# A list scheduler that lets the sums of VectorE and GpSimd exclude each other, and weight sums moved from the attention to the experts

## The chip, the cores and the metric

The kernel runs on one core of a Trainium2 chip. The metric is the device time of one execution in microseconds (us). Five engines work side by side in it, each with its own queue that is worked off in order: TensorE (PE in the profile, with its weight loads as PEld), VectorE (DVE), ScalarE (ACT), GpSimd (POOL) and SyncE (SP), which issues nearly all DMAs. They wait for each other through semaphores.

## The reference

Two transformer layers over 32 sequences of 128 positions with 512 features, all in fp32. The first layer normalises, adds a shift made from the condition, does attention with 16 heads of 64, and then a mixture of eight experts, in which every expert takes the 512 tokens that score highest for it. The second layer is an adaptive-norm block with attention (16 heads of 32) and an MLP of width 2048.

```python
# layer 0
h = _ln(x) + silu(t) @ W_ada.T
q, k, v = h @ Wqkv.T            # q and k normalised per head
x = x + softmax(q k^T / 8) v @ Wout.T
gate = softmax(tok @ Wgate.T);  vals, idx = top_k(gate.T, bs // 8)
y = gelu_tanh(_ln(tok[idx]) @ fc1[e].T) @ fc2[e].T
tok = tok.at[idx].add(y * vals)
# layer 1
n = layernorm(x) * (1 + scale) + shift
x = x + softmax(q k^T / sqrt(32)) v @ wo.T + bo
n = layernorm(x) * (1 + scale2) + shift2
x = x + gelu(n @ w1.T + b1) @ w2.T + b2
```

## The kernel before

**Stages.** The profiled execution goes through the attention of the first layer (0 to about 1000 us, called attention below), a short routing stage, eight experts (about 1110 to 1900 us, about 99 us each), and the second layer (about 1920 us to the end). The second layer works on eight blocks of four sequences. A block is two groups of two sequences (`group(g)`: norm, q/k/v, softmax, output projection, second norm), then `up(G, ...)` (first MLP matrix and gelu) and `down(G, ...)` (second MLP matrix). In the steady part a block takes about 161 us, and the attention of the next block is laid between the MLP products of this one.

**Fewer products, more sums.** Every large matrix product is made from 2x2 blocks with seven block products instead of four times two, at the price of sums of blocks on both sides. In the second layer's MLP this is done twice, one level inside the other: 49 products of four 128x128 matmuls each for `up` (`seeded`, L2794) and 49 for `down` (`chained`, L2876). So TensorE has less to do, and VectorE and GpSimd have much: sums of operands, sums of weights, and the combining of products. Sums of two tensors in SBUF go through `tt` (L1270): it gives the scheduler one way for VectorE (L1273) and, where allowed, one for GpSimd (L1274). In `down`, four such sums (`sums`, L2912) are made for each of seven outer products `o`; they are bound to GpSimd and held back by a gate on earlier products, `inner_done[-(2)]`: from the third outer product on, the sums may not begin before block product 7 of the chain two back is done.

**Weight sums of the last layer.** The summed forms of `w1` and `w2` don't depend on the data. They are made once, in 22 steps (`w1_outer`, `w2_outer`, `w1_inner`, `w2_inner`): each step loads four 128x512 pieces (`fetch`), makes four sums on GpSimd (`weight_forms`, through `tt`), and stores the results to DRAM (`put`), from where the second layer streams them (`piece`, L2696). That is 88 loads, 88 sums and 100 stores of 256 KB. In this kernel they belong to jobs 3 to 13, which lie in the first layer's attention.

**The order is planned.** All work is recorded as operations with an engine, an assumed duration, what they read and write, a priority (lower goes first) and a job number. `Sched.run` then plays them through in Python at build time: of all operations that could go it takes the one that can start earliest by its own clock, emits it, and so fixes the order of each engine's queue. Some operations may go to either of two engines; the plan chooses. On the chip nothing of the plan's times is left, only the order in each queue and the semaphores for true dependencies. The plan's durations are simple lines in the number of elements:

```python
def mm_us(n, count=1):
    return count * 2 * max(2 * n / 2400 + 0.0025, 0.11)
TR = 0.11
def dve_us(n, ptrs=0, half=False):
    return 0.15 + n / (1920 if half else 960) + 0.06 * ptrs
```

In the second layer a switch (`side_by_side`) gives `tt` other durations, for VectorE and GpSimd running beside each other: `0.15 + n / 700` and `0.16 + n / 400`, which is 0.88 and 1.44 us for 512 elements.

**Names for later.** `newton` (L419) makes an inverse root from the variance by an initial guess (L424) and three rounds of three tiny VectorE instructions (L428, L430, L432) on 128x2 or 128x4 elements. `normed` feeds it the variance (L464). `norm_T` (L2452) uses the result to scale rows (L2457), TensorE transposes them (L1243), and their columns are scaled and moved out of PSUM by VectorE or ScalarE (L2467, L2469). `chain_T` (L2565) makes the v and output projections; its results are taken up by L2588 and L2660 on VectorE. `comb` (L2721) and its copies on ScalarE (L2717) do so for `down`.

Of the kernel before, what the change touches and what calls it, by code (L numbers as in the profile page):

```python
# [14 lines left out]
ALU = mybir.AluOpType  # L15
# [171 lines left out]
class Op:  # L187
    __slots__ = ("alts", "prio", "job", "keep", "deps", "n", "ready", "next", "bufs", "lat", "done", "table", "seq", "mb")


class Sched:
# [7 lines left out]
    def __init__(self, window):  # L199
        self.ops, self.window = [], window  # L200
        self.load_exp = None

    def op(self, eng, us, fn, w=(), r=(), prio=0.0, job=0, keep=0, spare=0, lat=0.0, table=None, also=(), share=1.0):
# [4 lines left out]
        o = Op()  # L208
        o.alts = {eng: (us, fn)}
# [39 lines left out]
    def run(self):  # L249
# [10 lines left out]
        table = None  # L260
        live = set()
# [33 lines left out]
        while left:  # L295
            best = None
            for e in ENGINES:
# [3 lines left out]
                for o in cand[e]:  # L301
# [3 lines left out]
                    at = max(at, o.ready, free[e])  # L305
                    us = o.alts[e][0]
# [27 lines left out]
            free[e] = end  # L334
            lat = o.lat
# [24 lines left out]
def mm_us(n, count=1):  # L360

    return count * 2 * max(2 * n / 2400 + 0.0025, 0.11)


TR = 0.11
# [14 lines left out]
class Stage:  # L380
# [38 lines left out]
    def newton(self, v, n, name, pr, job):  # L419
# [7 lines left out]
        for _ in range(3):  # L427
            sch.op(DVE, us, lambda: nc.vector.scalar_tensor_tensor(t.t, y.t, -0.5, y.t, ALU.mult, ALU.mult),  # L428
                   w=[t], r=[y], prio=pr, job=job)
            sch.op(DVE, us, lambda: nc.vector.tensor_tensor(t.t, t.t, v.t, ALU.mult),  # L430
                   w=[t], r=[t, v], prio=pr, job=job)
            sch.op(DVE, us, lambda: nc.vector.scalar_tensor_tensor(y.t, t.t, 1.5, y.t, ALU.add, ALU.mult),  # L432
                   w=[y], r=[t, y], prio=pr, job=job)
        return y

    def guessed(self, mv, v, n, name, pr, job):
# [11 lines left out]
               w=[t], r=[y], prio=pr, job=job)  # L448
        sch.op(DVE, us, lambda: nc.vector.tensor_tensor(t.t, t.t, v.t, ALU.mult),
               w=[t], r=[t, v], prio=pr, job=job)  # L450
        sch.op(DVE, us, lambda: nc.vector.scalar_tensor_tensor(y.t, t.t, 1.5, y.t, ALU.add, ALU.mult),
               w=[y], r=[t, y], prio=pr, job=job)
# [701 lines left out]
def fast_kernel(ctx: ExitStack, tc: tile.TileContext, x, condT, mask, cols, w_ada, wqkv, wout, wout_p, wout_o, wgate,  # L1154
# [113 lines left out]
    side_by_side = [False]  # L1268

    def tt(o_, a_, b_, op_, n, w, r, pr, job, first=DVE, also=True):  # L1270

        shared = side_by_side[0]
        ways = {DVE: (DVE, 0.15 + n / 700 if shared else dve_us(n), lambda: nc.vector.tensor_tensor(o_(), a_(), b_(), op_)),  # L1273
                POOL: (POOL, 0.16 + n / 400 if shared else pool_us(n), lambda: nc.gpsimd.tensor_tensor(o_(), a_(), b_(), op_))}  # L1274
        sch.op(*ways[first], also=[ways[POOL if first == DVE else DVE]] if also else (), w=w, r=r, prio=pr, job=job)

    def recip(inv, ps, pr, job, at=None):
# [7 lines left out]
        if kept:  # L1285
# [5 lines left out]
               w=[inv], r=[t, y], prio=pr, job=job)  # L1291
# [951 lines left out]
    fence_b = stands(fence)  # L2243
    for e in range(E):
        up_done, near_end = expert(e, [fence_b] if e else [])

# [76 lines left out]
    def fetch(b_, src, r, pr, job):  # L2323
        sch.op(SP, 0.06, lambda: nc.sync.dma_start(b_.t, src), w=[b_], r=r, lat=4.0, prio=pr, job=job, spare=12)
# [68 lines left out]
    for n, step in enumerate(steps):  # L2393
        job = 3 + n // 2
# [659 lines left out]
```

## Time and profile before

The time is 3243.3 us (median of three runs, 3242.47 to 3243.88). The profiled execution took 3246.01 us, with a span of 3244.3 us from its first to its last instruction.

| stretch (us) | what | PE busy | DVE busy | ACT busy | POOL busy | GB/s |
|---|---|---|---|---|---|---|
| 0 to 1000 | attention, layer 0 | 962.5 | 786.3 | 364.3 | 235.6 | 124 |
| 1000 to 1120 | routing | 115.6 | 99.0 | 8.2 | 8.8 | 181 |
| 1120 to 1880 | experts | 759.1 | 515.0 | 174.5 | 495.1 | 111 |
| 1880 to 2000 | start of layer 1 | 117.4 | 59.1 | 40.8 | 6.3 | 62 |
| 2000 to 3140 | layer 1 | 1094.8 | 871.4 | 555.7 | 420.1 | 176 |
| 3140 to end | last block | 84.5 | 60.7 | 36.0 | 60.2 | 207 |

The columns are microseconds in which an engine had at least one instruction under way. A matmul's end is modelled, so a busy PE need not be PE at its peak; a gap in PE is a real gap. A group's mean duration can hide two cases, the instruction that ran alone and the one that was held up, so single instructions in order of time are the view that tells them apart.

### The profile page before, as it was taken

How to read it: one execution, taken by the hardware profiler on the slowest of the kernel's cores; microseconds unless marked ns; L12 is line 12 of the kernel's file. 1: busy time of each engine (PE TensorE's matmuls, PEld its weight loads, DVE VectorE, ACT ScalarE, POOL GpSimd, SP SyncE). 2: the span in 40 equal slices, each digit the busy share in tenths (PEclk: the TensorE clock that was granted, in tenths of full speed). 3: DMA queues.
4: the chain of work that ended last, by engine and by line, in shares of the span. 5: the costliest groups of instructions: out<-in, count | busy, mean ns of one | idle time of the engine just before them, and what ended most of it. 6: DMA issues, size and time to landing. Idle time of an engine off the chain costs nothing. (4 is left out here: it accounts for less than half of the span.)

```text
span 3244.3 us, 60361 instructions
## 1 busy us (share of the span) xinstructions
PE 3134.0 (97%) x22740; PEld 2549.3 (79%) x22740; DVE 2391.5 (74%) x4762; ACT 1179.4 (36%) x2972; POOL 1226.1 (38%) x920
## 2 busy tenths in 40 slices
PE   9999999999999999999999999999999999999997
PEld 5555555555557888888888888999898989898987
DVE  8877777788878897666676546786868686878675
ACT  3333333344431122211222214635353545454533
POOL 0323232221002157766676510615152525151536
PEclk9999999999999999999999999999999999999999
DMA  4234332444135333443333441646465646464666
GB/s 173 98 111 150 105 110 92 166 170 147 50 111 200 127 106 105 115 113 105 104 107 95 129 141 47 208 153 193 154 192 157 191 157 194 152 194 151 195 195 207
DMA packets 293453, 459.99 MB, mean 142 GB/s; under 512 B 29930, under 2 KB 111394, under 8 KB 293154
## 3 DMA queue, kind: packets, MB, share of 16 engines
q1 hardware_dynamic: 284498, 438.43, 42.0%
q0 software_dynamic: 7168, 16.91, 2.8%
q8 instruction: 182, 2.98, 0.4%
q14 instruction: 117, 0.96, 0.1%
q10 hardware_dynamic: 1488, 0.71, 0.1%
HBM read 383.44 MB, written 72.51 MB: 141 GB/s over the span
## 5 line engine op out<-in xcount | busy, mean ns | idle before, releaser
L1274 POOL TENSOR_TENSOR base<-base,base 128x512 f32<-128x512 f32 x336 | 466.0, 1401 | 813.6 <-DVE base L2845 473.3
L2876 PE MATMUL bank<-base,base 128*128 128x128 f32 x3072 | 375.1, 280 | 10.9 <-DVE base L2721 8.2
L1273 DVE TENSOR_TENSOR base<-base,base 128x512 f32<-128x512 f32 (+2 forms) x471 | 362.6, 788 | 30.3 <-ACT base L2737 9.5
L2876 PEld LDWEIGHTS bank<-base,base 128*128 128x128 f32 x3072 | 362.4, 195 | 22.9 <-DVE base L2721 11.1
L2794 PE MATMUL bank<-base,base 128*128 128x128 f32 x3088 | 371.8, 277 | 6.2 <-ACT bank L2755 4.9
L2794 PEld LDWEIGHTS bank<-base,base 128*128 128x128 f32 x3088 | 361.3, 193 | 9.6 <-ACT bank L2755 6.0
L2164 PE MATMUL d<-fc,h 128*128 128x256 f32 x992 | 218.9, 379 | 0.0
L2111 ACT ACTIVATE h<-h,prm 128x256 f32<-128x256 f32 x256 | 115.0, 500 | 257.2 <-DVE h L2105 257.1
L2164 PEld LDWEIGHTS d<-fc,h 128*128 128x128 f32 x992 | 188.0, 190 | 25.3
L1467 ACT ACTIVATE sq<-qk 128x512 f32<-128x512 f32 x128 | 81.7, 639 | 297.3 <-DVE qk L1505 257.3
L2100 PE MATMUL u<-gT,fc 128*128 128x256 f32 x768 | 178.6, 382 | 0.5 <-ACT gT L2063 0.5
L2804 ACT ACTIVATE base<-base,prm 128x128 f32<-128x128 f32 x512 | 164.1, 392 | 29.4 <-DVE base L2839 29.3
L2100 PEld LDWEIGHTS u<-gT,fc 128*128 128x128 f32 x768 | 147.2, 192 | 21.4 <-ACT gT L2063 0.9
L2839 DVE TENSOR_TENSOR base<-bank,base 128x512 f32<-128x512 f32 x96 | 65.9, 687 | 96.4 <-PE bank L2794 92.1
L2105 DVE TENSOR_TENSOR h<-v,u 128x512 f32<-128x512 f32 x128 | 86.5, 682 | 49.6 <-PE u L2100 47.9
L2100 PE MATMUL u<-tg,s 128*128 128x256 f32 x512 | 121.0, 379 | 0.9 <-DVE tg L1273 0.9
L1501 PE MATMUL q<-wqkv,hsb 128*128 128x512 f32 x240 | 113.5, 595 | 0.0
L2164 PE MATMUL d<-t,hs 128*128 128x256 f32 x512 | 113.4, 379 | 0.0
L1501 PE MATMUL q<-t,hsa 128*128 128x512 f32 x240 | 112.9, 592 | 0.0
L1501 PE MATMUL q<-wqkv,hT 128*128 128x512 f32 x240 | 111.6, 598 | 0.2 <-DVE hT L1602 0.2
L2845 DVE TENSOR_TENSOR base<-bank,base 128x512 f32<-128x512 f32 x120 | 81.7, 688 | 37.6 <-PE bank L2794 13.3
L2100 PEld LDWEIGHTS u<-tg,s 128*128 128x128 f32 x512 | 97.2, 190 | 14.4 <-issue 1.3
(1150 smaller groups left out, 6693.0 us busy)
## 6 DMA issues: line engine op xcount, KB each, us to landing
base<-w1i SPq DMA_DIRECT2D x224, 256.0 KB, 3.6
base<-w2i SPq DMA_DIRECT2D x224, 256.0 KB, 3.2
base<-w2s SPq DMA_DIRECT2D x168, 256.0 KB, 3.5
fc<-in_fc_dram SPq DMA_DIRECT2D x64, 512.0 KB, 4.8
fc<-in_fc_dram SPq DMA_DIRECT2D x32, 1024.0 KB, 5.6
base<-w1s SPq DMA_DIRECT2D x96, 256.0 KB, 2.9
base<-in_w_dram SPq DMA_DIRECT2D x72, 256.0 KB, 3.3
x<-in_x_dram SPq DMA_DIRECT2D x32, 256.0 KB, 3.7
```

Source lines behind the costliest of these rows:

```text
L1273: ways = {DVE: (DVE, 0.15 + n / 700 if shared else dve_us(n), lambda: nc.vector.tensor_tensor(o_(), a_(), b_(), op_)), POOL: (POOL, 0.16 + ...
L1274: POOL: (POOL, 0.16 + n / 400 if shared else pool_us(n), lambda: nc.gpsimd.tensor_tensor(o_(), a_(), b_(), op_))}
L1467: sch.op(ACT, act_us(D), lambda: nc.scalar.activation(sq.t, qk[i][j].t, AF.Square), w=[sq], r=[qk[i][j]], prio=pr, job=job)
L1501: nc.tensor.matmul(ps[m].t, lhs()[:, k, :], rhs[0](k), start=(k == 0), stop=(k == 1))
L2100: nc.tensor.matmul(ps[n].t[:, t, :], lhs()[:, k, t * P : (t + 1) * P], rhs.t[:, k, :], start=(k == 0), stop=(k == 1))
L2105: sch.op(DVE, dve_us(D), lambda: nc.vector.tensor_tensor(o_.t, a_.t, ps[n].t, ALU.add), w=[o_], r=[a_, ps[n]], prio=pr, job=job)
L2111: sch.op(ACT, act_us(HQ, 1), lambda t=t, c=c: nc.scalar.activation(o_.t[:, t, :], o_.t[:, t, :], AF.Gelu_apprx_tanh, bias=col("b1s", e * 1 ...
L2164: nc.tensor.matmul(ps[n].t[:, j, :], lhs[m].t[:, k, t * P : (t + 1) * P], rhs.t[:, 2 * m + k, :], start=(m == 0 and k == 0), stop=(m == NM ...
L2794: nc.tensor.matmul(b_.t[:, u, :], w_.t[:, u * P : (u + 1) * P], x_(), start=fresh and u == 0, stop=True, skip_group_check=True)
L2804: sch.op(ACT, act_us(S, 1), lambda k=k, u=u, c=c: nc.scalar.activation(o_[k].t[:, u * S : (u + 1) * S], o_[k].t[:, u * S : (u + 1) * S], A ...
L2845: sch.op(DVE, dve_us(D), lambda: nc.vector.tensor_tensor(d_[k].t, flat(src), flat(t_), ALU.add), w=[d_[k]], r=[src, t_], prio=po - 3000, j ...
L2876: nc.tensor.matmul(b_.t, x_()[:, k * S : (k + 1) * S], w_.t[:, k, :], start=fresh and k == 0, stop=True, skip_group_check=True)
```

## The change

1. `Op` gets a flag `port`. It is set on every `tt` sum, on the three instructions of each Newton round, on the row scaling in `norm_T`, on the second step of `recip` and on the sums with the output bias. From the job `lock_at` on (the second layer), the plan does not let a flagged operation of VectorE start before the last flagged operation of GpSimd has ended, and the other way round. It is a rule of the plan; no semaphore is added to the program for it.
2. `tt` loses the switch `side_by_side`: its durations are everywhere `dve_us(n)` and `0.2 + n / 480` (0.68 and 1.27 us for 512 elements). The smallest matmul is 0.112 instead of 0.11, a transpose 0.117 instead of 0.11.
3. The 22 weight steps move from jobs 3 to 13 to the first six experts, four steps to an expert, with low priority there. Each load (`fetch`) now also waits for the end of that expert's first half (`ups`).
4. Priorities and gates of the second layer have new values, `STREAM` (how many weight pieces may be loaded ahead) goes from 8 to 10, and the order comes out anew.

```diff
+        self.lock_at = math.inf
...
+        held = {DVE: 0.0, POOL: 0.0}
...
                     at = max(at, o.ready, free[e])
+                    if o.port and e in held and o.job >= self.lock_at:
+                        at = max(at, held[POOL if e == DVE else DVE])
...
             free[e] = end
+            if o.port and e in held:
+                held[e] = end
...
-    return count * 2 * max(2 * n / 2400 + 0.0025, 0.11)
+    return count * 2 * max(2 * n / 2400 + 0.0025, 0.112)
...
-TR = 0.11
+TR = 0.117
...
             sch.op(DVE, us, lambda: nc.vector.scalar_tensor_tensor(t.t, y.t, -0.5, y.t, ALU.mult, ALU.mult),
-                   w=[t], r=[y], prio=pr, job=job)
+                   w=[t], r=[y], prio=pr, job=job, port=True)
...
-        shared = side_by_side[0]
-        ways = {DVE: (DVE, 0.15 + n / 700 if shared else dve_us(n), lambda: nc.vector.tensor_tensor(o_(), a_(), b_(), op_)),
-                POOL: (POOL, 0.16 + n / 400 if shared else pool_us(n), lambda: nc.gpsimd.tensor_tensor(o_(), a_(), b_(), op_))}
-        sch.op(*ways[first], also=[ways[POOL if first == DVE else DVE]] if also else (), w=w, r=r, prio=pr, job=job)
+        ways = {DVE: (DVE, dve_us(n), lambda: nc.vector.tensor_tensor(o_(), a_(), b_(), op_)),
+                POOL: (POOL, 0.2 + n / 480, lambda: nc.gpsimd.tensor_tensor(o_(), a_(), b_(), op_))}
+        sch.op(*ways[first], also=[ways[POOL if first == DVE else DVE]] if also else (), w=w, r=r, prio=pr, job=job, port=True)
...
+    ups = []
     for e in range(E):
         up_done, near_end = expert(e, [fence_b] if e else [])
+        ups.append(up_done)
...
     def fetch(b_, src, r, pr, job):
-        sch.op(SP, 0.06, lambda: nc.sync.dma_start(b_.t, src), w=[b_], r=r, lat=4.0, prio=pr, job=job, spare=12)
+        sch.op(SP, 0.06, lambda: nc.sync.dma_start(b_.t, src), w=[b_], r=[*r, ups[job - RJ - 1]], lat=4.0, prio=pr, job=job, spare=12)
...
     for n, step in enumerate(steps):
-        job = 3 + n // 2
-        step(200 * job + 195, job)
+        e = n // 4
+        step(5000.0 + 1000 * e + 800, RJ + 1 + e)
...
-    side_by_side[0] = True
+    st.sch.lock_at = LJ
...
-        pn, pat, job = pr - (803) + (12) * sub, pr + (100) + (42) * sub, LJ + G
+        pn, pat, job = pr - (806) + (12) * sub, pr + (100) + (42) * sub, LJ + G
...
-    STREAM = (8)
+    STREAM = (10)
...
-        gate = inner_done[-(5):][:1]
+        gate = inner_done[-(10):][:1]
...
-               [(f, 0)], [op_, *inner_begun[-1:]], po - (75), job, DVE, False)
+               [(f, 0)], [op_, *inner_begun[-1:]], po - (22), job, DVE, False)
...
-        form(s1_, a21, a22, ALU.add, pr - (851))
-        form(s2_, s1_, a11, ALU.subtract, pr - (909))
-        form(a21, a11, a21, ALU.subtract, pr - (933))
+        form(s1_, a21, a22, ALU.add, pr - (785))
+        form(s2_, s1_, a11, ALU.subtract, pr - (839))
+        form(a21, a11, a21, ALU.subtract, pr - (953))
...
-                    tt(o_[0], a_[0], b_[0], op_, D, [o_[1]], [a_[1], b_[1], *(inner_done[-(2):][:1] if z > 1 else inner_done[-(13):][:1])], po - (16), job, POOL, NFORM)
+                    tt(o_[0], a_[0], b_[0], op_, D, [o_[1]], [a_[1], b_[1], *(inner_done[-(1):][:1] if z > 1 else inner_done[-(7):][:1])], po - (16), job, POOL, NFORM)
```

The two programs' queues compared: of 742 recorded TensorE steps in the first layer's attention 728 keep their order, of 1031 in routing and experts 1030, but of 1351 in the second layer only 720.

## The prediction

> **What bounds the kernel now.** I read the busy time by stage first. TensorE is busy 3134.0 of 3244.3 us, so no gain can come but from its 110.3 us of gaps. The table says where they lie (PE, PEld, DVE, ACT, POOL in this order): 37.5 us in the attention, 0.9 in the experts, 45.2 in the second layer and 19.8 in its last block.
>
> ```profile
> 0.00:1000.00 1000.00, 962.51 (x6592) 563.63 (x6596) 786.28 (x1682) 364.29 (x925) 235.60 (x199) 0.99 0.37 124
> 1120.00:1880.00 760.00, 759.12 (x3741) 669.57 (x3740) 515.04 (x769) 174.48 (x383) 495.11 (x361) 1.00 0.38 111
> 2000.00:3140.00 1140.00, 1094.82 (x10160) 1034.51 (x10152) 871.38 (x1737) 555.69 (x1440) 420.07 (x304) 0.99 0.57 176
> ```
>
> Next the waits of TensorE in 2000 to 3140 (us in total, times, longest). Nearly all are for VectorE:
>
> ```profile
> PE bank L1243 <- DVE base L2457: 22.0, 12, 3.4
> PE bank L2565 <- DVE base L2588: 7.8, 7, 2.7
> PE bank L2565 <- DVE base L2660: 5.7, 6, 1.0
> ```
>
> VectorE is busy 76% there, so it is late, not full. The timeline before one of these waits says why (start, duration, engine, line):
>
> ```profile
> 2603.85 3.88 POOL L1274 TENSOR_TENSOR base<-base,base 128x512 f32<-128x512 f32 x3 [6.66 <-PE bank L2876]
> ...
> 2604.38 0.77 DVE L464 TENSOR_SCALAR a_8v<-a_8mv 128x2 f32<-128x2 f32 x1
> ...
> 2605.50 1.00 DVE L428 SCALAR_TENSOR_TENSOR a_8t<-a_8y 128x2 f32<-128x2 f32 x1
> 2606.54 1.22 DVE L430 TENSOR_TENSOR a_8t<-a_8t,a_8v 128x2 f32<-128x2 f32 x1
> 2607.79 0.16 DVE L432 SCALAR_TENSOR_TENSOR a_8y<-a_8t,a_8y 128x2 f32<-128x2 f32 x1
> ...
> 2610.97 1.06 PE L1243 MATMUL bank<-ident,base 128*128 128x128 f32 x8 [2.73 <-DVE base L2457]
> ```
>
> Instructions on two elements take 1.00 and 1.22 us while a GpSimd sum runs, and 0.16 when none does. Each ends where a GpSimd sum ends. In this chain four are held up, by 0.60, 0.84, 1.06 and (at 2608.38) 1.06 us: 3.56 us, more than the 2.73 us that TensorE then stands still. The same happens in the attention, with a weight sum as the holder:
>
> ```profile
> 590.09 1.26 POOL L1274 TENSOR_TENSOR w1n_7f<-w1r,w1n_7f 128x512 f32<-128x512 f32 x1
> 590.19 1.18 DVE L428 SCALAR_TENSOR_TENSOR n_10t<-n_10y 128x2 f32<-128x2 f32 x1
> ...
> 596.20 1.26 POOL L1274 TENSOR_TENSOR w2r<-w2r,w2r 128x512 f32<-128x512 f32 x1
> 596.29 1.19 DVE L428 SCALAR_TENSOR_TENSOR n_10t<-n_10y 128x2 f32<-128x2 f32 x1
> ...
> 598.33 0.88 PE L1243 MATMUL tpq<-ident,qk 128*128 128x128 f32 x4 [3.34 <-DVE qk L1505]
> ```
>
> So the bound is TensorE, and its gaps are made by VectorE and GpSimd shutting each other out.
>
> **The change, part 1: weight sums leave the attention.** The 88 sums fill 117.5 us of GpSimd between 111 and 767 us. For every VectorE instruction overlapping one, I took its duration less the usual one of its line and shape: 54.3 us in all, 0.62 per weight sum. From 195 to 775 us TensorE has 21 gaps over 0.15 us, together 28.8 us. Counting for each gap no more than the hold-up by weight sums in the 8 us before it leaves 25.4 us. From 775 to 1000 us, with no weight sum, there is no such gap at all, so little else is late next. The TensorE order stays (728 of 742 steps). Against it: ten instructions net go from GpSimd to VectorE there, and the attention's own GpSimd sums still hold VectorE up. I take back 4 us: **-21 us**. The first 8.6 us of gaps (before 195 us) stay. SP loses 188 DMAs here, none of which TensorE waits for.
>
> **Part 2: the same work among the experts.** Sixteen sums to an expert (eight in the sixth) by 1.27 us are 20.3 us of GpSimd. The queue order puts most of them where GpSimd only waits for its four result sends:
>
> ```profile
> 1310.03 1.62 POOL L2196 DMA_INDIRECT acc<-y,idx  x1 [5.15 <-DVE y L2189]
> 1316.81 1.56 POOL L2196 DMA_INDIRECT acc<-y,idx  x1 [5.17 <-DVE y L2189]
> 1322.36 1.55 POOL L2196 DMA_INDIRECT acc<-y,idx  x1 [3.99 <-DVE v L2105]
> ```
>
> From 1304.9 to 1329.5 GpSimd is busy 6.5 of 24.6 us and VectorE 9.9; before w3b there are 7.0 us more. Room 25.1 us, need 20.3. A send may come 1.27 us later, and only the next expert's sums queue behind it. Over 98.7 us GpSimd goes from 69.8 to about 83 us (20.3 more, less some 5 sums that the plan moves to VectorE, by 1.38), VectorE from 70.0 to about 83 (5 by 0.68, and 16 by 0.62 of hold-up). Both stay under the expert's length.
>
> On SP an expert's 13 DMAs become up to 57, each load now waiting for the end of the expert's first half and each store for its sum; behind them in the queue stand the next expert's fc loads. `fc1_3` of the next expert is issued ahead of the first store, and the fc2 pieces, although behind stores, are read in the expert's second half, tens of us later. 49.3 MB over 590 us raise 109 GB/s to some 190; the second layer runs 256 KB loads at such rates in 3.2 to 3.6 us.
>
> Here the Trainium skill speaks against the move. "SBUF — State Buffer", section "Who interferes with whom", says that GpSimd and a VectorE instruction with two SBUF inputs contend for an exclusive lock, the later one blocked for the whole instruction. The rows above agree. Then the hold-up isn't removed but carried along. Lock time by undisturbed durations is 72% of an expert now (43 sums by 1.27 and 17.6 us of VectorE in 1300 to 1400) and would be 85 to 91%. By the rule alone the 54 us could come back and part 1 be worth about nothing. But a hold-up costs only where TensorE waits for it, and the trace has 0.9 us of that in 760. I follow the trace and put **+3 us**; bounds 0 and +80 (rival B).
>
> **Part 3: the second layer.** The gaps of one steady block (2384 to 2466 us) are 2.74, 0.98, 0.95, 0.62, 0.44 and 0.39: 6.1 us.
> - 2.74, the second norm. The new order leaves one GpSimd sum in the chain of Newton rounds instead of three or four. With a hold-up of 1.1 (1.22 less 0.16) the chain of 8.25 us becomes 8.25 - 3.56 + 1.1 = 5.8 against the six products (5.52 us) that cover it in both orders. Saved 2.2.
> - 0.95, the output projection behind L2660. Three small sums held up by 2.0 us stand ahead of it; the new order lays eight `down` products among its seven, where one stood. Saved 0.9.
> - 0.98, the v projection behind L2588, two sums of 0.68 taking 3.10. The new order again puts MLP products between. Saved 0.7.
> - The rest: 0.4 of 1.4.
>
> That is 4.2. I take 0.9 back, because the plan enforces nothing: on the chip GpSimd starts when its operands and gate are there. The plan doesn't flag L464 and L424 either, though L464 took 0.77 above. 3.3 by six blocks is 20; of the first block's 8.6 us (2006 to 2122) I take 4, of the last's 19.8 another 4: **-28 us**. The bounds are +5 (new gaps as large as the old) and -55.
>
> Two new costs are in this. The gate `inner_done[-(1)]` releases the four sums of an outer product one chain later: about three products (2.8 us) until the first is read, 1.27 us of sum plus up to 1.27 of hold-up. The plan lays other products between; TensorE would be what waits. And 25 evictions net go from ScalarE to VectorE, by 0.41 (L2467) 10 us over eight blocks, against some 250 us of slack. `STREAM` at 10 only loads earlier: no cost.
>
> **Sum.** -21 + 3 - 28 = -46 us. The profiled execution (3246.0 with the 1.7 us around its span) would take 3200; it lies 2.7 above the median, so against 3243.3 I predict 3197.
>
> **Rivals.**
> - *A: the new order of the second layer brings nothing.* For: the exclusion is only in the plan, and when GpSimd starts a little off, the collision is back elsewhere. Against: the new durations fit the rows (0.68 and 1.27; the old 0.88 and 1.44 fit no single row), and the collisions here repeat from block to block within 0.1 us, so an order can avoid them. 3243 - 21 + 3 = 3225.
> - *B: GpSimd becomes the experts' bound, and the kernel is slower.* Place: the queue of GpSimd in experts 0 to 5, with the stores on SP behind it. An expert has then some 51 sums on it. At 1.84 us each (the mean of the group `t<-fc,fc`; all take 1.38 now) they need 94 us, the sends and gathers 11, and 8.6 of its 28.9 us of waiting stay unfilled: 113 for an expert of 98.7. 5.5 experts by 14.6 are +80, and 3243 - 21 - 28 + 80 = 3274. It binds from a mean sum of 1.55 us, and outweighs the other 49 us from 1.73. Against: most sums fall where VectorE is busy 9.9 of 24.6 us.
> - *C: the attention keeps its gaps*, because something else is late at the same place: -6 instead of -21, 3212. Against: the gapless stretch after 775 us.
>
> **Chances.** The forecast 0.62, A 0.20, C 0.11, B 0.07. The forecast's own range is 3178 to 3214. To leave out no more than 2 in 10 I go to 3174 below, and to 3233 above, which takes in C and A. A measurement can tell 0.2% (6.5 us). Faster: forecast, C and nearly all of A, 0.90. Same: what is left of A and the lightest form of B, 0.04. Slower: 0.06.
>
> **What would show it.** Part 1: PE over 980 of the first 1000 us, no VectorE instruction on two elements at 1.18 us between 195 and 775 us save under the attention's own sums. Part 2: PE still without gaps among experts of about 99 us, GpSimd busy there some 83%; wrong, if PE waits there for GpSimd or a DMA. Part 3: a block of about 157.5 us instead of 161, and the wait L1243 <- L2457 well under 22 us. The prediction is wrong if the steady block keeps 6 us of gaps in other places.

## The result, and the profile after

The changed kernel takes 3228.75 us (median of five runs, 3226.28 to 3230.28), the kernel before 3243.3 beside it: a ratio of 0.9954, interval 0.994 to 0.9969. It is faster by 14.5 us where 46 were predicted. The profiled execution took 3228.02 us, its span is 3226.3.

Cut at two events that both traces have (the first transposes `tpg` of the first expert, the first transposes of the second layer), the spans compare so:

| stage | before | after | difference | predicted |
|---|---|---|---|---|
| attention and routing | 1110.1 | 1065.9 | -44.3 | -21 |
| experts | 811.9 | 864.2 | +52.4 | +3 |
| second layer | 1322.3 | 1296.2 | -26.1 | -28 |
| span | 3244.3 | 3226.3 | -18.0 | -46 |

So the small result is a sum of three large terms, and the middle one is wrong by 49 us. The busy time by stage of the kernel after (length, then PE, PEld, DVE, ACT, POOL with instruction counts, the granted clock of TensorE, DMA share, GB/s):

```profile
0.00:1000.00 1000.00, 991.69 (x6825) 594.23 (x6826) 780.91 (x1801) 368.51 (x937) 108.48 (x101) 1.00 0.26 85
1120.00:1880.00 760.00, 720.29 (x3462) 629.75 (x3462) 552.41 (x723) 161.06 (x359) 534.06 (x392) 0.97 0.55 167
2000.00:3140.00 1140.00, 1101.85 (x10264) 1039.33 (x10263) 840.54 (x1800) 555.73 (x1442) 392.85 (x298) 0.99 0.58 177
```

In the first row TensorE's gaps have shrunk from 37.5 to 8.3 us. In the second they have grown from 0.9 to 39.7 us, and the clock has fallen from 1.00 to 0.97, although neither VectorE (73% busy) nor GpSimd (70%) is full. The waits of TensorE among the experts (us in total, times, longest):

```profile
PE u L2104 <- DVE h L2109: 30.8, 6, 12.2
PE u L2104 <- DVE v L2109: 4.8, 2, 4.5
```

VectorE is late with the combining of the `u` products (L2109), a few times and by much. In the rows that follow a *send* is the indirect DMA `acc<-y,idx` with which GpSimd adds an expert's result to the tokens; `oh` and `val` pick the tokens of the next expert; `h` and `v` take up the combined `u` products (in PSUM) and then hold gelu results, of which `hs` are sums; `t` and `fc` are sums and pieces of the expert's second matrix (T1, T2 and fc2 in the text). The timeline of the worst place, after (start, duration, engine, line; "idle before" in brackets):

```profile
1411.93 1.56 POOL L2200 DMA_INDIRECT acc<-y,idx  x1 [4.42 <-DMA acc<-y,idx]
1412.96 1.83 POOL L1278 TENSOR_TENSOR w1n_4f<-w1n_4f,w1r 128x512 f32<-128x512 f32 x1
1413.11 0.68 DVE L2109 TENSOR_TENSOR h<-v,u 128x512 f32<-128x512 f32 x1
1413.70 19.20 DVE L1926 TENSOR_TENSOR oh<-iota_jb,lo 128x1024 bf16<-128x1024 bf16 x1
1414.19 1.83 POOL L1278 TENSOR_TENSOR w1r<-w1r,w1r 128x512 f32<-128x512 f32 x1
1415.42 1.83 POOL L1278 TENSOR_TENSOR w1n_4f<-w1r,w1n_4f 128x512 f32<-128x512 f32 x1
1416.65 5.46 POOL L1278 TENSOR_TENSOR t<-fc,fc 128x512 f32<-128x512 f32 x4
...
1421.54 5.42 POOL L1278 TENSOR_TENSOR t<-fc,t 128x512 f32<-128x512 f32 x4
1426.42 5.39 POOL L1278 TENSOR_TENSOR fc<-fc,fc 128x512 f32<-128x512 f32 x4
1432.83 0.67 DVE L2109 TENSOR_TENSOR h<-v,u 128x512 f32<-128x512 f32 x1
...
1433.56 2.93 PE L2104 MATMUL u<-gT,fc 128*128 128x256 f32 x6 [12.23 <-DVE h L2109]
```

One VectorE instruction (`oh`, 1.22 us when nothing holds it up) takes 19.20 us. In that time GpSimd goes through 15 sums, three weight sums and the twelve of T1, T2 and fc2. Look at starts and durations: 1412.96, 1414.19, 1415.42 are 1.23 us apart, yet each sum is shown as 1.83 long. Each begins 0.6 us before the one ahead of it has ended, and `oh`, which has two inputs in SBUF, gets in nowhere. (`h<-v,u` at 1413.11, whose `u` lies in PSUM, ran in its usual 0.68 us in between.) TensorE, waiting for `h`, stands still for 12.23 us. Gaps of 9.97 and 6.27 us follow at 1545 and 1657, behind VectorE instructions of 19.73 and 17.70 us.

The same state is there in the kernel before, at the same place, but it ends early:

```profile
1327.79 2.27 POOL L2196 DMA_INDIRECT acc<-y,idx  x1 [3.87 <-DVE h L2105]
...
1329.15 10.38 DVE L1922 TENSOR_TENSOR oh<-iota_jb,lo 128x1024 bf16<-128x1024 bf16 x2
...
1329.51 5.50 POOL L1274 TENSOR_TENSOR t<-fc,fc 128x512 f32<-128x512 f32 x4
1334.41 1.81 POOL L1274 TENSOR_TENSOR hs<-h,h 128x512 f32<-128x512 f32 x1
1336.30 2.14 POOL L1274 TENSOR_TENSOR hs<-hs,h 128x512 f32<-128x512 f32 x1
```

The first `oh` there takes 8.17 us: five sums overlap, then `hs<-hs,h`, which reads the sum directly before it, begins only after that has ended (1334.41 + 1.81 = 1336.22), and there VectorE is in: `hs<-hs,h`, held up in its turn, takes 2.14 us. I counted the boundaries between two GpSimd sums with no pause in the whole program, and took as overlapping those where the next sum begins over 0.1 us before the last has ended. In before 25 of 574 overlap, in after 75 of 502. Where a VectorE instruction was waiting, it was kept out at 21 of 21 overlapping boundaries in before and at 65 of 66 in after; at the others it got in (281 of 287 in before; the six left stand behind gathers, the indirect DMAs that fetch an expert's tokens). All of the overlapping stretches (7 in before, 15 in after) begin at a sum directly behind an indirect DMA that sends an expert's result; that sum starts 0.5 us before the end that the trace shows for the send.

Two more readings. The clock, in the same columns as the first fence, in and behind the 12.23 us gap:

```profile
1421.00:1433.00 12.00, 0.32 (x2) 0.00 (x0) 12.00 (x2) 0.00 (x0) 10.81 (x9) 0.64 0.85 269
1433.00:1440.00 7.00, 6.44 (x20) 5.31 (x21) 7.00 (x11) 2.29 (x5) 0.00 (x0) 0.64 0.00 0
1440.00:1450.00 10.00, 10.00 (x67) 8.98 (x66) 8.12 (x13) 5.88 (x14) 5.56 (x5) 1.00 0.16 35
```

From 1433 to 1440 TensorE works at 0.64, so by this estimate (7 us by 0.36) the gap costs 2.5 us more than its length. And the second layer. Its waits of TensorE from 2000 to 3140 us, and the chain of Newton rounds that the prediction looked at:

```profile
PE bank L1250 <- DVE base L2463: 16.1, 15, 4.4
PE bank L2882 <- DVE base L2727: 6.8, 7, 1.1
PE bank L2527 <- DVE base L2544: 4.4, 5, 0.9
```

```profile
2602.95 0.16 DVE L437 TENSOR_TENSOR a_8t<-a_8t,a_8v 128x2 f32<-128x2 f32 x1
2603.14 1.29 POOL L1278 TENSOR_TENSOR base<-base,base 128x512 f32<-128x512 f32 x1 [2.27 <-DVE a_8t L437]
2603.14 0.16 DVE L439 SCALAR_TENSOR_TENSOR a_8y<-a_8t,a_8y 128x2 f32<-128x2 f32 x1
2603.34 1.11 DVE L435 SCALAR_TENSOR_TENSOR a_8t<-a_8y 128x2 f32<-128x2 f32 x1
...
2608.04 0.65 PE L1250 MATMUL bank<-ident,base 128*128 128x128 f32 x4 [0.61 <-DVE base L2463]
```

One GpSimd sum is left in the chain and holds up one tiny instruction (1.11 instead of 0.16 us); the gap at the transposes is 0.61, not 2.73 us. A steady block takes 158.7 us, not 161. The whole layer, from its first transposes to the end, before and then after:

```profile
1922.00:3244.30 1322.30, 1256.22 (x11522) 1185.62 (x11522) 981.34 (x1972) 627.96 (x1634) 480.26 (x347) 0.98 0.54 168
1930.10:3226.30 1296.20, 1244.06 (x11522) 1173.45 (x11522) 936.17 (x2010) 616.36 (x1609) 441.21 (x333) 0.99 0.56 172
```

TensorE's gaps fell there from 66.1 to 52.1 us (by 13.9), and its busy time for the same 11522 matmuls by 12.2 us.

### The profile page after: what moved, and what is told of

Same layout as the page of the kernel before. It is cut to its first block, busy times and chain, and to the rows that moved or that the text cites. A ratio compares the mean times of both kernels' runs of the same rounds, so it can differ in the third digit from the quotient of the medians.

```text
span 3226.3 us, 60396 instructions
## 1 busy us (share of the span) xinstructions
PE 3122.8 (97%) x22740; PEld 2539.3 (79%) x22740; DVE 2389.7 (74%) x4834; ACT 1171.3 (36%) x2962; POOL 1124.2 (35%) x858
## 5 line engine op out<-in xcount | busy, mean ns | idle before, releaser
L1278 POOL TENSOR_TENSOR base<-base,base 128x512 f32<-128x512 f32 x330 | 437.5, 1337 | 854.4 <-DVE base L2851 278.1
L2882 PE MATMUL bank<-base,base 128*128 128x128 f32 x3080 | 369.0, 277 | 14.0 <-DVE base L2727 7.7
L2882 PEld LDWEIGHTS bank<-base,base 128*128 128x128 f32 x3080 | 355.0, 192 | 24.9 <-DVE base L2727 9.5
L1277 DVE TENSOR_TENSOR base<-base,base 128x512 f32<-128x512 f32 (+2 forms) x487 | 298.4, 636 | 18.7 <-PE bank L2882 3.6
L2109 DVE TENSOR_TENSOR h<-v,u 128x512 f32<-128x512 f32 x128 | 86.2, 681 | 45.9 <-PE u L2104 44.6
L2845 DVE TENSOR_TENSOR base<-bank,base 128x512 f32<-128x512 f32 x96 | 66.0, 687 | 72.1 <-PE bank L2800 56.8
L2727 DVE TENSOR_TENSOR base<-bank,base 128x128 f32<-128x128 f32 x168 | 47.7, 288 | 82.5 <-PE bank L2882 67.7
```

The costliest lines, as they stand in the source:

```text
L1277: ways = {DVE: (DVE, dve_us(n), lambda: nc.vector.tensor_tensor(o_(), a_(), b_(), op_)), POOL: (POOL, 0.2 + n / 480, lambda: nc.gpsimd.ten ...
L1278: POOL: (POOL, 0.2 + n / 480, lambda: nc.gpsimd.tensor_tensor(o_(), a_(), b_(), op_))}
L2109: sch.op(DVE, dve_us(D), lambda: nc.vector.tensor_tensor(o_.t, a_.t, ps[n].t, ALU.add), w=[o_], r=[a_, ps[n]], prio=pr, job=job)
L2845: sch.op(DVE, dve_us(D), lambda: nc.vector.tensor_tensor(d_[k].t, flat(src), first[k].t, ALU.add), w=[d_[k]], r=[src, first[k]], prio=po - ...
L2882: nc.tensor.matmul(b_.t, x_()[:, k * S : (k + 1) * S], w_.t[:, k, :], start=fresh and k == 0, stop=True, skip_group_check=True)
```

## Experiments

Theory S is that the weight sums, once behind the sends, shut VectorE out for whole runs of sums, and that this makes the experts slow. Its rivals put the loss elsewhere: the new durations of `tt`, the transfers, the loads on SP. All kernels stand beside runs of the kernel before; stages are cut as above and are those of the profiled execution (in T sums on VectorE 7 us above the median, in paced 6 us below it).

| kernel | median us | ratio to before, interval | experts | second layer | longest VectorE instruction among the experts, `w1a` left out |
|---|---|---|---|---|---|
| before | 3242 to 3243 | | 811.9 | 1322.3 | 8.2 |
| after | 3228.75 | 0.9954, 0.994 to 0.9969 | 863.1 | 1296.2 | 19.7 |
| steps back | 3219.32 | 0.9926, 0.9909 to 0.9942 | 812.1 | 1296.2 | 8.2 |
| steps alone | 3231.49 | 0.9966, 0.9953 to 0.9978 | 842.7 | 1320.3 | 18.3 |
| no sends | 3173.77, one run | | 808.9 | 1295.1 | 3.1 |
| paced | 3215.11 | 0.9917, 0.9901 to 0.9934 | 846.4 | 1294.2 | 15.5 |
| no exclusion | 3295.03 | 1.0164, 1.0147 to 1.0181 | 868.6 | 1361.6 | 20.0 |
| pause, last sends | 3229.38 | 0.9957, 0.994 to 0.9974 | 865.9 | 1294.2 | 5.2 |
| pause, all sends | 3265.73 | 1.0071, 1.0055 to 1.0088 | 905.9 | 1294.6 | 3.2 |
| hs on GpSimd | 3224.16 | 0.9942, 0.9925 to 0.9958 | 859.8 | 1296.9 | 21.9 |
| T sums on VectorE | 3205.52 | 0.9876, 0.9857 to 0.9894 | 848.0 | 1296.0 | 6.3 |
| T sums chained | 3209.22 | 0.9897, 0.988 to 0.9913 | 842.3 | 1297.9 | 6.3 |
| dependent pair | 3189.83 | 0.9838, 0.9821 to 0.9854 | 827.5 | 1293.8 | 3.3 |
| before, with the pair | 3243.06 | 1.0003, 0.9995 to 1.0012 | 811.9 | 1319.3 | 3.3 |

**Steps back: the change without its part on the weight steps.**

```diff
-        e = n // 4
-        step(5000.0 + 1000 * e + 800, RJ + 1 + e)
+        job = 3 + n // 2
+        step(200 * job + 195, job)
```

> The changed kernel with the 22 weight steps put back into the attention (jobs 3 to 13, no wait for an expert's first half); all else as changed. Theory S (the experts lose what they lose because VectorE is shut out during unbroken runs of GpSimd sums, and only the moved sums make these runs): the experts go back to about 99 us each without TensorE gaps, the attention goes back to its 29 us of gaps and its spells of half clock, and the second layer keeps its gain: span from the first transposes of layer 1 to the end 1295 us, total 3243 - 26 = 3217. Rival R (the experts are slower because of the new durations in tt, which let the plan shift sums between VectorE and GpSimd): the experts stay above 100 us each and the total is 3240 or more.

It took 3219.32 us, as S expected: faster than the whole change. The stages, in the columns of the first fence:

```profile
0.00:1000.00 1000.00, 960.02 (x6584) 561.92 (x6588) 799.44 (x1691) 364.02 (x926) 225.19 (x189) 1.00 0.37 124
1120.00:1880.00 760.00, 759.26 (x3740) 669.32 (x3739) 523.94 (x792) 174.30 (x384) 466.22 (x339) 1.00 0.37 111
```

The attention has its gaps again, the experts have none. So the new durations of `tt` alone don't slow the experts, and moving the sums gains about 44 us in one stage and loses 52 in the next.

**Steps alone: the kernel before with only the weight steps moved** (and the gate that goes with them).

> The kernel before with the 22 weight steps moved to the experts (and the wait for an expert's first half), all else as before. Theory S: the attention ends about 42 us earlier, the second layer takes its old 1321 us from its first transposes to the end, and the experts lose some 50 us because runs of 10 and more GpSimd sums stand behind the last result send of an expert; total 3243 - 42 + 50 = about 3250. Rival R: the old durations in tt keep the sums where they were, the experts lose less than 10 us, total about 3210.

It took 3231.49 us, between the two expectations. The experts lose 31 us, not 52: the older durations give another order in them, with VectorE shut out for 18.3 us once and 10.9 us once. How much is lost depends on what the plan happens to put behind the sends.

**No sends: after, with the 32 indirect DMAs of the experts' results left out**, so the expert outputs are missing from the sum.

> The changed kernel with the 32 result sends of the experts (indirect DMAs on GpSimd that add into acc) left out, so the experts' results are missing; the order of all queues stays. It asks what shuts VectorE out for 19 us. Theory S1 (an indirect DMA on GpSimd right ahead of a run of sums puts the run into a state in which the next sum is begun before the last has ended, so the lock is never free): without sends the sums of the runs take 1.27 us instead of 1.83, VectorE gets in between two of them, no instruction of VectorE in the experts takes over 6 us, and TensorE has under 10 us of gaps there. Theory S2 (any long run of sums that wait for nothing shuts VectorE out): instructions of 13 to 20 us remain, and so do gaps of 6 to 12 us.

3173.77 us. The sums take 1.27 us again, and the expert row is nearly gapless while the weight traffic stays:

```profile
1120.00:1880.00 760.00, 759.70 (x3738) 666.34 (x3737) 499.13 (x769) 169.59 (x374) 505.56 (x369) 1.00 0.50 168
```

With the same loads, stores and sums at 168 GB/s there is no gap, so neither SP's queue nor the weight transfers make the loss. The order of every engine's other instructions is that of after. So the loss needs the sends; whether it is their place ahead of the sums or their own transfers, this run can't say (the runs with chained sums and with the pair, below, keep the transfers).

**Paced: after, with the T1, T2 and fc2 sums in three portions, each behind a tiny GpSimd sum that reads a gelu result.**

> The changed kernel with the T1, T2 and fc2 sums of experts 1 to 7 recorded after the first, second and third quarter of the expert's first half, each set behind a tiny GpSimd instruction (128x1) that reads a gelu result of that quarter: GpSimd then really has to wait there, and no run goes on through all twelve sums. Theory S (runs that nothing breaks): no VectorE instruction in the experts takes over 9 us, TensorE has under 8 us of gaps there, the experts take 99 to 101 us each, total 3228 - 45 = about 3183. Rival G (GpSimd is simply full, 85 to 90% of an expert): waiting makes it later still, the gaps stay or grow, total 3228 or more.

3215.11 us, a part of what was expected. The tiny sums were meant to make GpSimd wait; but when VectorE is late already, what they read had mostly been there for long. They took 0.7 to 0.8 us within the overlapping run, which went on: `oh` still took 14.45 and 15.45 us. So a tiny instruction that has nothing to wait for doesn't end the state.

**No exclusion: after, planned without the new rule**, all constants and due times kept.

```diff
-    st.sch.lock_at = LJ
```

> The kernel after, planned without the rule that VectorE's and GpSimd's sums exclude each other; every constant, due time, hold and the place of the weight steps stay as the change has them. The rule acts from the second layer on only, so attention and experts should be as in after (experts 863 us, VectorE's longest instruction 19 us). Theory X (the rule itself makes the second layer's 25 us): the layer goes back to about 1320 us, 3253 in all. Rival Y (the due times and holds found by the new search make it, the rule only served to find them): the layer stays within 5 us of 1296, 3229 in all. Rival Z (due times found under one model are wrong under the other): over 1325 us, slower than before.

3295.03 us: rival Z. The second layer takes 1361.6 us, 65 more than with the rule and 39 more than before. In the waits from 2000 to 3140 us VectorE's combining of products is late everywhere:

```profile
PE bank L2881 <- DVE base L2726: 21.3, 19, 2.5
PE bank L1250 <- DVE base L2462: 15.9, 7, 2.3
PE bank L2626 <- DVE base L2726: 13.9, 7, 2.1
```

So the due times found with the rule are only good with it. What the rule with due times searched without it would give was not tried.

**Pause behind sends.** Behind the last two sends of each of the first seven experts (the expectation speaks of the last alone; the kernel paused behind both) GpSimd zeroes a column of the tile just sent, for which it must wait until the transfer has read it:

```diff
                         in_=yt[h].t, in_offset=None, compute_op=ALU.add)
+                    nc.gpsimd.memset(yt[h].t[:, 0:1], 0.0)
```

> The kernel after in the same order on every engine, but directly behind the last send of each of the first seven experts GpSimd zeroes one column of the tile just sent; it can do so only when the transfer has read that tile, so GpSimd really waits there (about 4.5 us) before its 12 to 15 sums. Nothing is left out: the tile is not used again before it is rewritten. Theory S2 (the sums shut VectorE out for their whole run only because they begin right behind a send; after a real wait they let it in between two sums): VectorE's longest instruction among the experts falls from 19.7 to under 8 us, the sums' mean from 1.83 to about 1.27 us, the PE gaps of 12, 10 and 6 us go, experts about 815 us, 3180 in all. Rival T (it is the length of the unbroken run of sums, not what stands ahead of it): VectorE's instructions of 13 to 19 us stay, 3229. Rival U (GpSimd's added waits make the sums late for TensorE): the gaps come back as waits of the products for GpSimd's t sums, 3205 to 3230.

Half of S2 came true: of 75 overlapping boundaries 7 are left, all behind the earlier sends, and VectorE's longest instruction behind a send is 5.2 us. The time is 3229.38 us all the same. The timeline shows what came in its place:

```profile
1311.04 0.09 POOL L2205 MEMSET y<- 128x1 f32 x1 [5.00 <-DMA acc<-y,idx]
1311.17 0.69 DVE L2109 TENSOR_TENSOR v<-v,u 128x512 f32<-128x512 f32 x1 [5.96 <-POOL y L2205]
```

VectorE's next result goes into the buffer of a sent tile, so VectorE waits for that send too, and for the memset behind it. Such waits sum to 28.5 us among the experts, and TensorE's gaps there are 35.5 us, in shorter pieces. With the pause behind every send it is worse, 3265.73 us:

> As the run before, but the pause stands behind every send of the experts (four or five an expert), not the last of each alone. Theory S2: also the shorter hold-ups of 5 to 8 us behind the earlier sends go, VectorE's longest instruction under 5 us; as TensorE has hardly a gap left for them, the time is that of the run before within 3 us, unless GpSimd's waits (32 of 4.5 us, 144 us, on an engine that has 30% free, 230 us) are felt: then up to 20 us slower than it by waits of products for GpSimd.

There its upper guess (20 us slower) was too low: the second kernel is 36 us slower than the first. Taking the overlap away helps nothing if a wait for the transfer is put in its place.

The theory now needed a sharper form (V): the state begins at a sum right behind a send, and ends at the first sum that has to wait, be it only for the sum directly before it. Four kernels were run for it.

**hs on GpSimd**: the first quarter's hs sums of an expert bound to GpSimd.

> The kernel after, with the four sums hs of an expert's first quarter (m=0) bound to GpSimd as the plan before had most of them, from the second expert on. They then stand behind the three weight sums that follow the last send and ahead of the twelve sums of T1, T2 and fc2, and the second hs sum reads the first one's result. Theory V (the state in which VectorE is shut out begins at a sum right behind a send and ends at the first sum that has to wait, be it only for the sum directly before it): VectorE's longest instruction falls from 19.7 to 5 to 7 us, the PE gaps of 12, 10 and 6 us go, experts about 820 us, 3185 in all. Rival T (the length of the run of sums decides): the run is longer by four, VectorE's longest is 20 us or more, experts 863 to 875, 3226 to 3240.

3224.16 us, by its total nearer to rival T than to V, but the timeline shows why. At 1202, 1420 and 1528 us two hs sums follow each other, the second reading the first, and VectorE is let in after 5.5, 7.0 and 5.7 us. At 1634 us the plan put T sums between the two, 17 sums overlap, and VectorE is shut out for 21.85 us; TensorE stands still for 11.1.

**T sums on VectorE**: twelve sums of an expert taken off GpSimd.

> The kernel after, with the twelve sums of T1, T2 and fc2 of experts 2 to 8 bound to VectorE, not GpSimd (12 x 0.69 = 8.3 us an expert more on VectorE, 12 x 1.23 = 14.8 us less on GpSimd); the plan then puts more of the hs sums on GpSimd. Theory V and rival T both expect that no run of more than eight sums stands behind a send: VectorE's longest instruction 5 to 9 us, no PE gap over 4 us, experts 820 to 830 us, 3185 to 3195 in all. If VectorE's load is what binds (rival W: 552 of 760 us and 8 us an expert more), the gaps stay as many short ones of 1 to 2 us and the time stays near 3215.

3205.52 us. No VectorE instruction behind sends is over 6.3 us, but TensorE still has gaps up to 6.6 us, behind a VectorE with more to do. At the longest gap, before 1433.8 us, `h<-v,u` stands behind one T sum held up over the three sums behind a send (4.62 us) and behind the other T sums, so V and W both take their part here, and this run doesn't separate them.

**T sums chained: same engine, same number of sums, another order.** T1 and T2 alternate, so that every T2 reads the sum directly before it.

```diff
+                def pair(hs=hs):
+                    nc.gpsimd.tensor_tensor(T1.t[:, hs, :], Bf[1, 2].t[:, hs, :], Bf[1, 1].t[:, hs, :], ALU.subtract)
+                    nc.gpsimd.tensor_tensor(T2.t[:, hs, :], Bf[2, 2].t[:, hs, :], T1.t[:, hs, :], ALU.subtract)
```

> The kernel after, same sums on the same engine and as many in a run; only their order among the twelve is changed from T1 x4, T2 x4, fc2 x4 to T1, T2, T1, T2, ... fc2 x4, so that a T2 sum reads the result of the sum directly before it and has to wait for it (experts 2 to 8). Theory V: the run ends its overlapping state at the first T2, five sums behind the last send; VectorE's longest instruction 5 to 8 us (from 19.7), the three long PE gaps go, 3185 in all. Rival T (length of the run): no change, 19 us, 3229 in all.

3209.22 us. The timeline at the place of the 19.20 us:

```profile
1414.49 8.04 DVE L1926 TENSOR_TENSOR oh<-iota_jb,lo 128x1024 bf16<-128x1024 bf16 x2
...
1415.07 1.73 POOL L1278 TENSOR_TENSOR w1r<-w1r,w1r 128x512 f32<-128x512 f32 x1
1416.30 1.72 POOL L1278 TENSOR_TENSOR w1n_4f<-w1r,w1n_4f 128x512 f32<-128x512 f32 x1
1417.52 1.71 POOL L2043 TENSOR_TENSOR t<-fc,fc 128x512 f32<-128x512 f32 x1
1419.31 2.14 POOL L2044 TENSOR_TENSOR t<-fc,t 128x512 f32<-128x512 f32 x1
1421.42 2.25 POOL L2043 TENSOR_TENSOR t<-fc,fc 128x512 f32<-128x512 f32 x1
```

The sums overlap up to the first T1 (1417.52 + 1.71 = 1419.23); T2 starts at 1419.31, and the first `oh` ends after 5.83 us. As many sums follow each other as in after, so this rejects the rival that the length of the run decides. The time fell short of the expected 3185: hold-ups of 3.5 to 6.3 us behind the earlier sends are left, and 18.8 us of gaps.

**Dependent pair: behind every send of after, a memset of a 128x1 scratch tile and a sum that reads it.** Nothing waits for a transfer.

```diff
                         in_=yt[h].t, in_offset=None, compute_op=ALU.add)
+                    nc.gpsimd.memset(p1.t, 0.0)
+                    nc.gpsimd.tensor_tensor(p2.t, p1.t, p1.t, ALU.add)
```

> The kernel after, with two tiny GpSimd instructions behind every send of the experts: a memset of a 128x1 scratch tile and a sum that reads it (and so waits for it); nothing waits for a transfer. Theory V: every run of sums behind a send starts in the normal state; sums' mean 1.27 us, VectorE's longest instruction among the experts 5.5 us (w1a, as in the kernel without sends) or less, experts 812 to 820 us, 3178 to 3186 in all. Rival T, or if a wait so short doesn't do: as after, 19 us, 3229. If it is the send's transfer itself that keeps VectorE out for its 5 to 8 us: VectorE's longest stays at 6 to 8 us behind sends, 3200.

3189.83 us, the fastest kernel here that computes everything: 1.6% under before, and 0.9838 / 0.9954 = 0.988 of after. Timeline and stage row:

```profile
1411.68 1.58 POOL L2202 DMA_INDIRECT acc<-y,idx  x1 [3.85 <-DMA acc<-y,idx]
1412.70 0.69 POOL L2205 MEMSET p<- 128x1 f32 x1
1413.46 2.35 DVE L1926 TENSOR_TENSOR oh<-iota_jb,lo 128x1024 bf16<-128x1024 bf16 x2
1413.47 1.25 POOL L2206 TENSOR_TENSOR p<-p 128x1 f32<-128x1 f32 x1
1414.69 2.25 POOL L1278 TENSOR_TENSOR w1n_4f<-w1n_4f,w1r 128x512 f32<-128x512 f32 x1
1416.91 1.71 POOL L1278 TENSOR_TENSOR w1r<-w1r,w1r 128x512 f32<-128x512 f32 x1
```

```profile
1120.00:1880.00 760.00, 748.03 (x3632) 656.47 (x3631) 499.57 (x743) 162.06 (x360) 567.32 (x461) 1.00 0.57 176
```

Where one `oh` took 19.20 us, two now take 2.35 together. None of the 532 boundaries between sums overlaps by over 0.1 us, and VectorE is busy 52.8 us less in this stretch than in after, with the same sends, the same weight sums and the same order of all other instructions. Whether the memset or the sum alone would do was not tried.

A weaker form is left: the longest VectorE instruction in the stage is `w1a` with 5.7 us, held over four sums in a row behind a gather, which is an indirect DMA too. These sums overlap by no more than 0.05 us, and yet VectorE gets in only at the first sum that waits for the one before it. No pair stands there, and TensorE doesn't wait for it; the kernel without sends shows the same (5.55 us). The experts take 827.5 us, 15.6 more than before. TensorE's gaps from 1120 to 1880 us are 12.0 us, where before had 0.9; VectorE waits 21.2 us there for tiles still being sent. Whether these make the gaps was not tried.

**The control: the same pair in the kernel before.**

> The kernel before with the same two tiny GpSimd instructions (a memset of a 128x1 scratch tile and a sum that reads it) behind every send of the experts; a control for the run of after with them. Theory V: the overlapping state goes here too (25 of 574 boundaries between two GpSimd sums in before), VectorE's longest instruction behind the sends falls from 8.2 us to under 5.7, but TensorE waited for none of it (0.9 us in the whole stage), so the time is that of before within 0.2%, 3236 to 3250. If the pair gained by something else than VectorE's hold-up (rival: it orders the queue or lightens the transfers), before gains by it too, 10 us or more.

3243.06 us, no difference. VectorE's busy time among the experts falls from 515.0 to 480.0 us, and nothing is gained, because TensorE waited for none of it. So the pair brings nothing of its own; what it gains in after goes with VectorE's hold-up.

## Why the prediction was wrong

- **Part 2, "I follow the trace and put +3 us"**: this step failed; it is +52.4 us. TensorE's gaps in the experts grew from 3.5 to 42.9 us, and about 10 of the other 13.0 us are half clock behind them. The trace's 0.9 us of waits in the experts said that VectorE's hold-ups there were harmless as they stood, up to 8.2 us each. It did not say how long they become when more sums stand behind a send. I priced a hold-up at 0.62 us per weight sum, the size seen in the attention, where no send stands ahead. The rule of the Trainium skill weighed there ("SBUF — State Buffer", "Who interferes with whom") gave the right sign. But as I read it, a later instruction is held for one instruction of the other engine, so it allows one sum's length; the runs show up to 17 sums. That the 54 us which "could come back" by that rule lie so near to 52.4 is chance: they came as a few long gaps and low clock, not as 88 short hold-ups.
- The clue was in the profile of before, in the row cited for rival B (count, then busy time in us and mean in ns):

```profile
L1274 POOL TENSOR_TENSOR t<-fc,t 128x512 f32<-128x512 f32 x32 | 42.0, 1342 | 0.0
L1274 POOL TENSOR_TENSOR t<-fc,fc 128x512 f32<-128x512 f32 x28 | 38.5, 1837 | 0.0
```

28 sums of a mean 1.837 us make 51.4 us, but the busy time is 38.5 us: these instructions overlap. The group above, of the same shape, has 32 by 1.342, 42.9 us, and is busy 42.0.
- "Room 25.1 us, need 20.3" counted GpSimd's free time beside the sends as the safe place. It is the place where a sum does most harm.
- **Rival B** came true in place (GpSimd's queue in the experts) and in that the experts got slower; the kernel as a whole did not. Its price, +80, was too high and its mechanism wrong: GpSimd is 70% busy and binds nothing. A mean sum over 1.73 us isn't what decides, but which VectorE instruction is shut out how long.
- **Rivals A and C.** That 3225, the number of rival A, lies near the measured 3228.75 is chance: the second layer did gain, and the experts lost. C did not come: the attention lost nearly all its gaps.
- **Part 1, -21**: right mechanism, too small; it is -44.3. TensorE's gaps in the first 1000 us fell by 29.2 where 21 were put: the first 195 us kept theirs (7.4 of 8.6), as expected, but behind them only 0.8 of 28.8 us is left, so the 4 us taken back for the attention's own sums weren't needed. The gaps of the routing stage, left out of the sum, fell by another 3.1. The clock was left out too. In before it was 0.86 over the 12 us from 62, and 0.66, 0.83 and 0.83 over the 10 us from 196, 469 and 596, which is 8.5 us lost, some 0.5 of it inside a gap; after shows 1.00 in all four. The rest, about 4 us, I can't attribute. After, TensorE is busy 991.7 us of the first 1000; over 980 was the test.
- **Part 3, -28**: it is -26.1, but that the number fits is in part luck. The sum was one of gaps alone, and TensorE's gaps in the layer fell by only 13.9 us. A steady block still has 4.4 of its 6.1 us, where 2.8 was expected: the norm's 2.73 became 0.61, but gaps of about 1 us appeared at L2527, L2882 and L1250. The first block gave the 4 us put for it, the last stretch none. The other 12.2 us are busy time of TensorE for the same matmuls. Half-clock spells sum to 41 us there before and 20 after, and half of that is lost: 20.6 and 10.1 us, a term that the sum left out. The steady block takes 158.7 us where 157.5 was expected, and the wait L1243 <- L2457 went from 22.0 to 16.1 us (L1250 <- L2463 after). The chain shows the one sum that was expected. The gaps listed for a steady block are those of 2384 to 2546 us; "2466" is a slip.
- The SP side was read right: the fc loads land after 7.6 and 8.5 us instead of 4.8 and 5.6, and no wait of TensorE among the experts is for one; the kernel without sends has 0.3 us of gaps from 1120 to 1880 us, with the same loads.

## What to carry to other kernels

Before you give an engine's idle time more work, ask what stands directly ahead of it in that queue, and whom the work shuts out. If an instruction group's count times its mean exceeds its busy time, its instructions overlap, and an engine that such instructions hold up one at a time may get no turn until something in that queue has to wait. An engine's lateness that costs nothing in one order is no measure of what it costs in another: price it by its longest stretch, and add the clock that TensorE loses behind each long gap.

## What the runs showed of the hardware

- GpSimd sums that follow such a send, with no wait between, start every 1.23 us, last 1.7 to 1.8 us each, and keep VectorE's instructions with two SBUF inputs out for the whole run (19.2 us over 15 sums, 21.85 us over 17). A sum that has to wait for the one directly before it ends this; a wait for an older result, already there, doesn't (in after 24 of the 251 sums with a wait on GpSimd's own semaphore still overlap). Two tiny dependent instructions behind each send, 0.9 us together where nothing held them up, took away every such overlap; the weaker hold-ups behind gathers stayed.
- Why a send starts it, no run shows. The Trainium skill, "GPSIMD Engine Reference", "Instruction dispatch", says that GpSimd's eight cores each go on to the next instruction when their share is done, while what waits on an instruction's semaphore waits for all of them. Cores put out of step by the send, so that VectorE finds no moment between two sums, would fit; the trace has no single cores, so this is a guess.
- TensorE's half-clock spells are 3.41 us long or a multiple of it (the last of a trace is cut off by its end), up to 13.65 us around the 12.23 us gap (part of it in the gap itself), and in a trace their starts lie whole multiples of 3.413 us apart (the first five of before 39, 80, 37 and 150 times). Every gap over 4 us in before and after brought one. Of the seven gaps of 2.7 us in the second layer of before four did and three did not, and three spells followed gaps of 1.3 to 1.5 us. "TensorE: Matmul & The Clock Gate", "What's actually happening", gives a window of about 3.4 us that runs on whatever the kernel does, which agrees.
